# Softmax denominators in a four-batch attention layer: row sums by matmuls with ones, or by 32x32 transposes and row sums on VectorE

## The chip, the cores and the metric

The kernel runs on one core of one Trainium2 chip. The metric is the device time of one execution in microseconds (us). The engines that matter are TensorE (PE in the profile; its weight loads are listed apart as PEld), VectorE (DVE), ScalarE (ACT), GpSimd (POOL), and SyncE (SP), which issues nearly all the DMAs. Each engine executes its own instructions in the order in which the program issued them, so an instruction that has to wait holds up everything behind it on the same engine.

## The reference

The layer is a group norm, a projection to queries, keys and values, attention over 48x48 = 2304 positions with 8 heads of 64 channels, an output projection and a residual sum, for 4 images of 512 channels.

```
hn = _group_norm(x, gn_scale, gn_bias)
qkv = jnp.einsum('oc,bchw->bohw', qkv_w, hn) + qkv_b[None, :, None, None]
qkv = qkv.reshape(b, 3, num_heads, d, t).astype(jnp.float16)
q, k, v = (qkv[:, 0], qkv[:, 1], qkv[:, 2])
scale = jnp.asarray(1.0 / math.sqrt(math.sqrt(d)), dtype=jnp.float16)
w = jnp.einsum('bhct,bhcs->bhts', q * scale, k * scale)
w = jax.nn.softmax(w, axis=-1)
a = jnp.einsum('bhts,bhcs->bhct', w, v).astype(jnp.float32)
a = a.reshape(b, c, hh, ww)
out = jnp.einsum('oc,bchw->bohw', proj_w, a) + proj_b[None, :, None, None]
return x + out
```

The change is about the denominator of the softmax: for each head and query, the sum of the exponentials over all 2304 keys.

## The kernel before

**Tiling.** Heads are worked on in pairs, one head on partitions 0 to 63 and the other on 64 to 127; there are 16 pairs (4 images, 4 pairs each). The queries of a pair are cut into five blocks, four of 512 columns and one of 256. The keys are cut into 18 tiles of 128. A unit is one step of the main loop (L1332): the scores of three 1024-column tiles for a block, their exponentials, and so on. A block of 512 has six units, one of 256 has three, so there are 27 units to a pair and 432 in all, and 80 blocks.

**One iteration n of the main loop**, in order of issue:

- `scores(n)` (L920): matmuls of keys and queries into a PSUM tile `ps` (three buffers), and three exponentials on ScalarE (L939) from it into an fp16 tile `p` with room for three units.
- `add(n-1)` (L968): VectorE adds the unit's `p` to the block's running fp16 sum `acc` (L986, 3072 columns). At the last unit of a block the three thirds are joined into the first one by two further additions (L989). After this, `acc` holds, for each of the 128 partitions (keys modulo 128), 1024 partial sums: two heads by 512 queries.
- `values(n-2)` (L942): matmuls of `p` and the values into the only `av` bank. After a block's last unit VectorE copies the bank out (`avx`, L966).
- `fill(n)` (L1283): a ration of other work that keeps TensorE busy: projections for the queries and keys of later pairs (L709, evacuated at L719), for the values (L760, L768), the output projection (L837, L864). All of these chains use one PSUM bank, `pw` (`ps_w` has one buffer), so the first matmul of a chain waits until VectorE has evacuated the chain before. A chain of 512 columns of a projection is issued in two halves over two iterations, and the evacuation comes at the end of the second. `fill` also releases small VectorE tasks at certain stages: statistics of the next image (L608) and its normalization (L660).

**The sums**, for a block whose last unit is n-2. In iteration n+1, ahead of `scores`, `add_up` (L992) multiplies `acc` by a matrix of ones on TensorE: two matmuls of 512 columns (four of 256 for the narrow block), which put each head's sum on all 64 of its partitions, into the `av` bank. `rows` (L1021) copies that bank to SBUF on VectorE (`slx`, L1025) and sends one row of each head by DMA to a [128, 2, 4] tile `sums`. In iteration n+2, after `values`, GpSimd compares the sums with two limits (`check_sums`, L1040), and VectorE takes the reciprocals (`invert`, L1050), which go by DMA to a row in DRAM. In n+3 `spread` reads that row back, broadcast over partitions (`ib`), and in n+4 `divide` multiplies `avx` by it on GpSimd (L1073). In iteration n+1 `fill` is issued ahead of `values`, since the next block's `values` need the `av` bank that `slx` still has to be copied out of.

The last three of the 80 blocks (`soon` and the very last one, L1326) have a path of their own and keep the matmuls with ones.

Of the kernel before, what the change touches and what calls it, by code (L numbers as in the profile page):

```python
# [12 lines left out]
F32 = mybir.dt.float32  # L13
# [4 lines left out]
ALU = mybir.AluOpType  # L18
AX = mybir.AxisListType
# [7 lines left out]
P = 128  # L27
# [6 lines left out]
BEHIND = 2  # L34
# [8 lines left out]
QB = 512  # L43
QBLOCKS = [(o, min(QB, T - o)) for o in range(0, T, QB)]
# [4 lines left out]
SUM_MIN, SUM_MAX = 256.0, 60000.0  # L49
# [418 lines left out]
def fast_path(  # L468
# [12 lines left out]
    nc = tc.nc  # L481

    RES = NC
    const = ctx.enter_context(tc.tile_pool(name="const", bufs=1))
    xpool = ctx.enter_context(tc.tile_pool(name="xpool", bufs=1))
    qkp = ctx.enter_context(tc.tile_pool(name="qkp", bufs=3))
# [3 lines left out]
    work = ctx.enter_context(tc.tile_pool(name="work", bufs=2))  # L490
    small = ctx.enter_context(tc.tile_pool(name="small", bufs=2))
    dram = ctx.enter_context(tc.tile_pool(name="dram", bufs=4, space=DRAM))
# [7 lines left out]

    SPARE = {(1, 2): lambda c: ("res", RES), (1, 3): lambda c: (f"a32_{c}", 1)}

# [71 lines left out]
    ones16 = const.tile([P, D], F16, name="ones16")  # L574
    nc.gpsimd.memset(ones16, 1.0)

    fine = const.tile([P, 2 * QB // P], F32, name="fine")
    nc.gpsimd.memset(fine, 1.0)

# [14 lines left out]

    SQ = 32
    NGROUP = SQ // GROUP  # L600
    moments = const.tile([P, 3, SQ], F32, name="moments")
    nc.gpsimd.memset(moments, 1.0)
# [303 lines left out]

    open_sums = set()
    av, acc, pts, avx, sums, rowd, ibs = {}, {}, {}, {}, {}, {}, {}  # L910

    stream = []
# [7 lines left out]
    def scores(u):  # L920
        g, j, k, _ = u
        o, n = QBLOCKS[j]
        per = QB // n
        qt, kt = qk[g]
        pt = ppool.tile([P, BURST, 2, QB], F16, tag="p", name=f"p_{g}_{j}_{k}")
        for r in range(BURST):
            ps = ps_s.tile([P, 2, QB], F32, tag="ps", name=f"ps_{g}_{j}_{k}_{r}")
            for a in range(per):
                i = (k * BURST + r) * per + a
                for h in range(2):  # L930
                    rows = slice(h * D, (h + 1) * D)
                    nc.tensor.matmul(  # L932
                        ps[:, h, a * n : (a + 1) * n],
                        kt[rows, bass.ts(i, P)],
                        qt[rows, o : o + n],
                        start=True,
                        stop=True,
                    )
            nc.scalar.activation(pt[:, r], ps, AF.Exp)  # L939
        pts[u] = pt  # L940
# [27 lines left out]
    def add(u):  # L968

        g, j, k, last = u  # L970
        pt = pts[u]
        if k == 0:
            acc[g, j] = [pt]
            return
        if j >= NQ - 2 and g == NG - 1 and (last or j == NQ - 1):
            acc[g, j].append(pt)
            return
        before = acc[g, j][0]
        if k == 1:
            acc[g, j] = [  # L980
                work.tile(
                    [P, BURST, 2, QB], F16, tag="acc", bufs=1, name=f"acc_{g}_{j}"
                )
            ]
        t = acc[g, j][0]
        nc.vector.tensor_tensor(t, before, pt, ALU.add)  # L986
        if last:
            for r in range(1, BURST):
                nc.vector.tensor_tensor(t[:, 0], t[:, 0], t[:, r], ALU.add)  # L989
            acc[g, j] = [t[:, :1]]  # L990

    def add_up(g, j, bank=None, more=False):  # L992


        o, n = QBLOCKS[j]
        per = QB // n
        sl = bank
        if bank is None:
            sl = ps_av.tile([P, QB], F32, tag="av", name=f"sl_{g}_{j}")
        steps = [  # L1000
            (t, r, a)
            for t in acc.pop((g, j))
            for r in range(t.shape[1])
            for a in range(per)
        ]
        for i, (t, r, a) in enumerate(steps):
            for h in range(2):
                lo = h * D
                nc.tensor.matmul(  # L1009
                    sl[lo : lo + D, :n],  # L1010
                    ones16,
                    t[:, r, h, a * n : (a + 1) * n],
                    start=(i == 0 and (g, j) not in open_sums),
                    stop=(i == len(steps) - 1 and not more),
                )
        if more:
            acc[g, j] = []
            open_sums.add((g, j))
        return sl

    def rows(g, j, sl):  # L1021

        o, n = QBLOCKS[j]
        sx = work.tile([P, QB], F32, tag="rows", name=f"slx_{g}_{j}")
        nc.vector.tensor_copy(sx[:, :n], sl[:, :n])  # L1025
        sm = small.tile([P, 2, QB // P], F32, tag="sums", name=f"sums_{g}_{j}")
        for h in range(2):
            nc.sync.dma_start(sm[:, h, : n // P], sx[h * D : h * D + 1, :n])
        sums[g, j] = sm
        return sx  # L1030

    def divide_here(g, j, source, products, engine):
        o, n = QBLOCKS[j]
# [6 lines left out]
    def check_sums(g, j):  # L1040
        n = QBLOCKS[j][1]
        sm = sums[g, j][:, :, : n // P]
        ok = fine.rearrange("p (h i) -> p h i", h=2)[:, :, : n // P]
        for op, limit in ((ALU.is_ge, SUM_MIN), (ALU.is_le, SUM_MAX)):
            t = small.tile([P, 2, QB // P], F32, tag="in", name=f"in_{g}_{j}")
            t = t[:, :, : n // P]
            nc.gpsimd.tensor_scalar(t, sm, limit, None, op)  # L1047
            nc.gpsimd.tensor_tensor(ok, ok, t, ALU.mult)

    def invert(g, j):  # L1050
        n = QBLOCKS[j][1]
        per = n // P
        inv = small.tile([P, 2, QB // P], F32, tag="inv", name=f"inv_{g}_{j}")
        nc.vector.reciprocal(inv[:, :, :per], sums[g, j][:, :, :per])
        row = dram.tile([2, QB], F32, tag="row", name=f"row_{g}_{j}")
        nc.sync.dma_start(
            row[:, :n].rearrange("h (p i) -> p h i", i=per), inv[:, :, :per]
        )
        rowd[g, j] = row
# [103 lines left out]
    for b in range(B):  # L1163
        g = b * NPAIR
# [163 lines left out]
    def block_at(n):  # L1328

        return stream[n][:2] if ended(n) and n not in soon else None  # L1330

    for n in range(end):  # L1332
        now[0] = n
        while loads and loads[0][0] <= n:
            loads.popleft()[1]()
        summed = block_at(n - BEHIND - 1)
        if summed:
            rows(*summed, add_up(*summed))
        wanted(stream[n][0])
        scores(stream[n])  # L1340
        if n > 0:
            add(stream[n - 1])
        if summed:

            fill(n)
        if n >= BEHIND:
            values(stream[n - BEHIND])
        if block_at(n - BEHIND - 2):
            check_sums(*block_at(n - BEHIND - 2))
            invert(*block_at(n - BEHIND - 2))  # L1350
        if block_at(n - BEHIND - 3):
            spread(*block_at(n - BEHIND - 3))
        if block_at(n - BEHIND - 4):

            divide(*block_at(n - BEHIND - 4))
        if not summed:
            fill(n)
        if n - BEHIND in soon:
            g, j = stream[n - BEHIND][:2]
            sx = rows(g, j, add_up(g, j))  # L1360
            if n - BEHIND == soon[1]:
                divide_here(g, j, sx, avx[g, j], nc.gpsimd)
        if n - BEHIND - 1 == soon[0]:
            check_sums(g, j)
            invert(g, j)
        if n - BEHIND - 2 == soon[0]:
            spread(g, j)
            divide(g, j)
    g, b, j = NG - 1, B - 1, NQ - 1
    n = QBLOCKS[j][1]  # L1370
# [5 lines left out]
    sl = ps_s.tile([P, 2, QB], F32, tag="ps", name="sl_last")[:, 0, :]  # L1376
# [2 lines left out]
    values(stream[-1])  # L1379
    add_up(g, j, sl)  # L1380

    every = fine.shape[1] + n
    fines = work.tile([P, QB], F32, tag="rows", name="fines")[:, :every]
    ok = work.tile([P, QB], F32, tag="avx", name="ok")[:, :n]
    nc.scalar.copy(fines[:, :n], sl[:, :n])
    nc.gpsimd.tensor_scalar(ok, fines[:, :n], SUM_MIN, None, ALU.is_ge)
    nc.gpsimd.tensor_scalar(fines[:, :n], fines[:, :n], SUM_MAX, None, ALU.is_le)
    nc.gpsimd.tensor_tensor(fines[:, :n], fines[:, :n], ok, ALU.mult)
    nc.gpsimd.tensor_copy(fines[:, n:], fine)
    divide_here(g, j, sl, av[0], nc.vector)  # L1390
    att32(b, j, LAST)
    while beside or loads:
# [10 lines left out]
    good = small.tile([P, 1], F32, tag="good", bufs=1, name="good")  # L1403
    pf = small_bank("count")[:1, :1]
    for i, (evacuate, store) in enumerate(ends_of):
        if i == NC - 1:
            nc.vector.tensor_reduce(good, fines, AX.X, ALU.add)
            nc.tensor.matmul(pf, good, ones, start=True, stop=True)
        if i == len(rest) - 1:
            nc.vector.tensor_scalar(flag, pf, P * every - 0.5, None, ALU.is_lt)  # L1410
        evacuate()
        store(nc.scalar if i % 2 else nc.sync)
# [57 lines left out]
```

## Time and profile before

| what | value |
|---|---|
| timed runs | median 1619.79 us of 3, 1617.14 to 1620.52 |
| span of the profiled execution, first to last instruction | 1617.1 us |
| the profiled execution's time around its span | none is listed apart; the lowest timed run (1617.14) equals the span |
| chain that ended last, by engine | PE 91%, ACT 4%, issue 2%, DVE 1%, DMA 1% |
| exponentials, L939 | 1296 of 1027 ns |
| additions to `acc`, L986 | 270 of 1798 ns and 79 of 1749 ns |
| joins, L989 | 156 of 695 ns |
| HBM | 49 GB/s over the span |

Busy time of an engine is the union of its instructions' times; the matmuls overlap each other in the pipeline, so the mean of one is longer than its share of the time. The chain of work is followed back from the last instruction: it names the engine that the end waited for. Starts in a timeline are us from the start of the span.

### The profile page before, as it was taken

The page shows a single profiled execution, that of the slowest core. Times are in us where ns is not written, and L with a number is a line of the kernel's source. Part 1 is how long each engine was busy: PE and PEld are TensorE (multiplying, and loading weights), DVE is VectorE, ACT ScalarE, POOL GpSimd, SP SyncE. Part 2 cuts the span into 40 slices and gives each one's busy share as a digit, 9 for nine tenths or more (in the row PEclk, how much of TensorE's full clock was granted, in tenths as well). Part 3 has the DMA queues.
Part 4 walks back from the last instruction along what each step waited for, and adds up shares of the span by engine and source line. Part 5 has one row for each costly group of instructions (what it writes and reads, how often), then busy time and mean ns, then how long its engine had stood idle before and what let it go on. Part 6 is the DMA issues. An engine that isn't in the chain of part 4 may idle for free.

```text
span 1617.1 us, 28315 instructions
## 1 busy us (share of the span) xinstructions
PE 1583.4 (98%) x11500; PEld 695.5 (43%) x11500; DVE 1136.2 (70%) x1302; ACT 1282.8 (79%) x1398; POOL 298.4 (18%) x419
## 2 busy tenths in 40 slices
PE   6999999999999999999999999999999999999996
PEld 2533434443333534555333353455533334434544
DVE  6267668866666678986666666898666666767775
ACT  3077777888888888888887887887888888888894
POOL 1001102211121222212111121111211131111211
PEclk9999999999999999999999999999999999999999
DMA  7002020000000023511000002352100000016424
GB/s 221 1 14 66 11 64 24 18 14 11 14 18 14 12 65 118 154 54 28 14 11 18 14 12 61 100 158 73 31 14 12 14 18 15 15 24 191 121 62 132
DMA packets 94898, 82.11 MB, mean 51 GB/s; under 512 B 50852, under 2 KB 60964, under 8 KB 94756
## 3 DMA queue, kind: packets, MB, share of 16 engines
q1 hardware_dynamic: 92724, 78.35, 17.3%
q8 instruction: 92, 1.51, 0.4%
q10 hardware_dynamic: 1904, 1.84, 0.4%
q14 instruction: 50, 0.41, 0.1%
q0 software_dynamic: 128, 0.01, 0.0%
HBM read 60.70 MB, written 19.17 MB: 49 GB/s over the span
## 4 chain that ended last, share of the span: by engine, by line
PE 91%; ACT 4%; issue 2%; DVE 1%; DMA 1%; POOL 0%; SPq 0%; ACTq 0%; DVEq 0%; POOLq 0%
PE pqk L709 29%; PE ps L932 19%; PE av L957 19%; PE pv L760 16%; PE pr L837 7%; ACT p L939 3%; PE ps L709 1%; PE sl L1009 1%; ACT a L831 1%; DMA x<-x_dram 1%; DVE acc L986 0%; DMA sums<-slx 0%; DVE r L860 0%; DMA row<-inv 0%; DMA ib<-row 0%
## 5 line engine op out<-in xcount | busy, mean ns | idle before, releaser
L939 ACT ACTIVATE p<-ps 128x1024 f16<-128x1024 f32 x1296 | 1231.9, 1027 | 299.9 <-PE ps L932 299.3
L986 DVE TENSOR_TENSOR acc<-acc,p 128x3072 f16<-128x3072 f16 x270 | 485.3, 1798 | 75.5 <-ACT p L939 74.7
L709 PE MATMUL pqk<-x,wqkv 128*64 128x512 f32 (+1 forms) x2464 | 519.3, 551 | 0.0
L932 PE MATMUL ps<-q,k 64*128 64x512 f16 (+1 forms) x2880 | 359.5, 358 | 6.2 <-ACT p L939 5.3
L957 PE MATMUL av<-p,v 128*64 128x512 f16 (+1 forms) x2880 | 361.0, 364 | 0.4 <-DVE slx L1025 0.3
L760 PE MATMUL pv<-wqkv,x 128*64 128x256 f32 x2304 | 268.6, 380 | 0.0
L709 PEld LDWEIGHTS pqk<-x,wqkv 128*64 128x64 f32 x2464 | 168.9, 137 | 224.2 <-issue 166.8
L1047 POOL TENSOR_SCALAR in<-sums 128x8 f32<-128x8 f32 (+1 forms) x158 | 116.6, 738 | 795.0 <-DMA sums<-slx 788.7
L932 PEld LDWEIGHTS <-k 64*128 64x128 f16 x2880 | 107.3, 94 | 286.1 <-issue 238.1
L957 PEld LDWEIGHTS <-v 128*64 128x64 f16 x2880 | 131.9, 109 | 210.8 <-issue 166.6
L1073 POOL TENSOR_TENSOR att<-avx,ib 128x512 f16<-128x512 f32 (+1 forms) x78 | 120.0, 1539 | 450.4 <-DMA ib<-row 406.3
L760 PEld LDWEIGHTS pv<-wqkv,x 128*64 128x64 f32 x2304 | 160.1, 137 | 92.8 <-issue 4.5
L986 DVE TENSOR_TENSOR acc<-p,p 128x3072 f16<-128x3072 f16 x79 | 138.2, 1749 | 0.0
L837 PE MATMUL pr<-a,whi 128*128 128x512 f32 (+1 forms) x312 | 122.2, 399 | 4.6 <-DVE r L860 3.2
L837 PE MATMUL pr<-a,wlo 128*128 128x512 f32 (+1 forms) x312 | 114.4, 373 | 0.0
L989 DVE TENSOR_TENSOR acc<-acc 128x1024 f16<-128x1024 f16 x156 | 108.4, 695 | 5.4
L719 DVE TENSOR_SCALAR q<-pqk,bqkv 128x512 f16<-128x512 f32 (+1 forms) x79 | 55.0, 696 | 80.4 <-PE pqk L709 79.8
L719 DVE TENSOR_SCALAR k<-pqk,bqkv 128x512 f16<-128x512 f32 (+1 forms) x75 | 52.2, 696 | 78.1 <-PE pqk L709 78.0
L768 DVE TENSOR_TENSOR v<-pv,bv 128x512 f16<-128x512 f32 x72 | 49.7, 691 | 81.1 <-PE pv L760 80.9
L966 DVE COPY avx<-av 128x512 f32<-128x512 f32 (+1 forms) x79 | 50.6, 641 | 66.4 <-PE av L957 66.4
L864 DVE SCALAR_TENSOR_TENSOR r<-pr,bproj,r 128x512 f32<-128x512 f32 (+1 forms) x80 | 54.9, 694 | 43.6 <-PE pr L837 43.0
L837 PEld LDWEIGHTS pr<-a,whi 128*128 128x128 f32 x312 | 58.5, 187 | 41.9 <-issue 18.7
(62 smaller groups left out, 448.8 us busy)
## 6 DMA issues: line engine op xcount, KB each, us to landing
r<-x_dram SPq DMA_DIRECT2D x72, 256.0 KB, 3.0
out_dram<-r SPq DMA_DIRECT2D x69, 256.0 KB, 2.1
ib<-row SPq DMA_DIRECT2D x126, 128.0 KB, 3.0
x<-x_dram SPq DMA_DIRECT2D x62, 256.0 KB, 4.3
x<-x_dram SPq DMA_DIRECT2D x16, 128.0 KB, 4.8
sums<-slx SPq DMA_DIRECT2D x128, 2.0 KB, 2.1
ib<-row SPq DMA_DIRECT2D x30, 64.0 KB, 3.0
wqkv<-qkv_wT_dram SPq DMA_DIRECT2D x2, 768.0 KB, 6.9
```

The lines of the kernel that those rows point to most:

```text
L709: nc.tensor.matmul(pw[0][lo : lo + D, :n], wqkv[:, c, w0 + lo : w0 + lo + D], hn[b, c, j], start=(c == 0), stop=(c == NC - 1),)
L719: nc.vector.tensor_scalar(qk[g][part][:, o : o + n], pw[0][:, :n], bqkv[:, col : col + 1], SCALE, ALU.add, ALU.mult,)
L760: nc.tensor.matmul(pw[0][lo : lo + D, a, :], hn[b, c, i * P // QB][:, at + lo : at + lo + D], wqkv[:, c, 2 * C + half * C // 2 :][:, : C / ...
L837: nc.tensor.matmul(ps[:, :n], w[:, c, bass.ts(m, P)], at32[b, j, c], start=(i == 0), stop=(i == len(steps) - 1),)
L864: nc.vector.scalar_tensor_tensor(xt[:, i], places[i], bias, xt[:, i], ALU.add, ALU.add)
L932: nc.tensor.matmul(ps[:, h, a * n : (a + 1) * n], kt[rows, bass.ts(i, P)], qt[rows, o : o + n], start=True, stop=True,)
L939: nc.scalar.activation(pt[:, r], ps, AF.Exp)
L957: nc.tensor.matmul(av[0][lo : lo + D, :n], vv[b, pr // 2][:, i, pr % 2 * P + lo : pr % 2 * P + lo + D], pt[:, r, h, a * n : (a + 1) * n], ...
L986: nc.vector.tensor_tensor(t, before, pt, ALU.add)
L989: nc.vector.tensor_tensor(t[:, 0], t[:, 0], t[:, r], ALU.add)
L1047: nc.gpsimd.tensor_scalar(t, sm, limit, None, op)
L1073: nc.gpsimd.tensor_tensor(atts[g][:, o : o + n], avx.pop((g, j))[:, :n], ibs.pop((g, j))[:, :n], ALU.mult,)
```

## The change

For 77 of the 80 blocks the matmuls with ones, the copy `slx` and the two DMAs of rows go. In their place:

- `turn`, in iteration n, after `scores(n)` and ahead of the copy `avx`: VectorE transposes the 128 x 1024 fp16 sums in 32x32 squares, into the second third of the same `acc` tile (free after the joins).
- `fold`, at the end of iteration n, after `fill`: VectorE sums each run of 32 columns of the transposed tile (128 x 1024 fp16 into 128 x 32 fp32). Four DMAs bring the four groups of 32 partitions of the result side by side on 32 partitions (`quarters`, 32 x 128).
- `invert_turned`, in iteration n+2, where `invert` stood: VectorE sums the four quarters (and, for the narrow block, its two halves), takes 32 reciprocals on 32 partitions, and transposes the 32x32 square; for the narrow block GpSimd first sets the unused columns to one. Two DMAs instead of one write the row to DRAM. The comparisons on GpSimd follow here, on 32 partitions.

`spread` and `divide` stay where they were; so does the order of `fill` and `values` in iteration n+1.

```diff
     for n in range(end):
         now[0] = n
...
         summed = block_at(n - BEHIND - 1)
-        if summed:
-            rows(*summed, add_up(*summed))
         wanted(stream[n][0])
         scores(stream[n])
+        if block_at(n - BEHIND):
+            turn(*block_at(n - BEHIND))
         if n > 0:
             add(stream[n - 1])
         if summed:
...
         if block_at(n - BEHIND - 2):
-            check_sums(*block_at(n - BEHIND - 2))
-            invert(*block_at(n - BEHIND - 2))
+            invert_turned(*block_at(n - BEHIND - 2))
...
         if not summed:
             fill(n)
+        if block_at(n - BEHIND):
+            fold(*block_at(n - BEHIND))
```

The new functions:

```python
    def turn(g, j):

        nc.vector.transpose(
            t_turned(g, j).rearrange("p h n -> p (h n)"),
            acc[g, j][0][:, 0].rearrange("p h n -> p (h n)"),
        )

    def fold(g, j):

        part = small.tile([P, SQ], F32, tag="part", name=f"part_{g}_{j}")
        nc.vector.tensor_reduce(
            part,
            t_turned(g, j).rearrange("p h (c k) -> p (h c) k", k=SQ),
            AX.X,
            ALU.add,
        )
        del acc[g, j]
        quarters = small.tile([SQ, P // SQ, SQ], F32, tag="quarters", name=f"qs_{g}_{j}")
        for p in range(P // SQ):
            nc.sync.dma_start(quarters[:, p, :], part[bass.ts(p, SQ), :])
        sums[g, j] = quarters

    def t_turned(g, j):
        return acc[g, j][0][:, 1]

    def invert_turned(g, j):
        n = QBLOCKS[j][1]
        per, cols = QB // n, n // SQ
        quarters = sums.pop((g, j))
        sm = small.tile([SQ, 2, cols], F32, tag="tsum", name=f"tsum_{g}_{j}")
        nc.vector.tensor_reduce(
            sm,
            quarters.rearrange("i p (h a c) -> i h c p a", h=2, a=per),
            AX.XY,
            ALU.add,
        )
        inv = small.tile([SQ, SQ], F32, tag="tinv", name=f"tinv_{g}_{j}")
        if 2 * cols < SQ:
            nc.gpsimd.memset(inv[:, 2 * cols :], 1.0)
        nc.vector.reciprocal(inv[:, : 2 * cols], sm.rearrange("i h c -> i (h c)"))
        back = small.tile([SQ, SQ], F32, tag="tback", name=f"tback_{g}_{j}")
        nc.vector.transpose(back, inv)
        row = dram.tile([2, QB], F32, tag="row", name=f"row_{g}_{j}")
        for h in range(2):
            nc.sync.dma_start(
                row[h, :n].rearrange("(c i) -> c i", i=SQ),
                back[h * cols : (h + 1) * cols, :],
            )
        rowd[g, j] = row
...
```

The rest of the change keeps books: the joined `acc` tile is kept whole, so that its second third can be written, and the flags of the comparisons get 32 more columns on 32 partitions.

## The prediction, made before the changed kernel was run

> **What bounds the kernel now.** I read the busy shares and slices first, then the groups by shape, then one block's end in the timeline, then the busy time by stage.
>
> ```profile
> PE 1583.4 (98%) x11500; PEld 695.5 (43%) x11500; DVE 1136.2 (70%) x1302; ACT 1282.8 (79%) x1398; POOL 298.4 (18%) x419
> DVE  6267668866666678986666666898666666767775
> ```
>
> TensorE is busy without a gap between the first and the last slice, so each microsecond taken from it can shorten the run. VectorE has 30% to spare on average, but three stretches with an 8 or 9. The groups by shape (busy us, mean ns | idle before) show what goes and the nearest prices:
>
> ```profile
> L1025 DVE COPY slx<-sl 128x512 f32<-128x512 f32 x64 | 43.8, 684 | 19.1 <-PE sl L1009 19.1
> L1009 PE MATMUL sl<-acc,ones 128*64 128x512 f16 x132 | 25.2, 383 | 0.2 <-DVE avx L966 0.2
> L1054 DVE RECIPROCAL inv<-sums 128x8 f32<-128x8 f32 x63 | 12.3, 195 | 0.0
> L622 DVE STREAM_TRANSPOSE turned<-moments 128x96 f32<-128x96 f32 x7 | 2.2, 307 | 0.2
> L645 DVE STREAM_TRANSPOSE cols<-both 128x64 f32<-128x64 f32 x7 | 1.7, 245 | 0.2
> L1407 DVE TENSOR_REDUCE good<-fines 128x1 f32<-128x264 f32 x1 | 0.4, 418 | 0.0
> ```
>
> The timeline (start, length) of a block's end near 1180 us:
>
> ```profile
> 1176.08 0.82 PE L932 MATMUL ps<-q,k 64*128 64x512 f16 x6
> ...
> 1177.78 0.69 DVE L966 COPY avx<-av 128x512 f32<-128x512 f32 x1 [0.95 <-PE av L957]
> ...
> 1179.22 0.38 PE L1009 MATMUL sl<-acc,ones 128*64 128x512 f16 x2
> 1179.44 0.75 DVE L719 TENSOR_SCALAR k<-pqk,bqkv 128x512 f16<-128x512 f32 x1 [0.97 <-PE pqk L709]
> 1179.54 0.82 PE L932 MATMUL ps<-q,k 64*128 64x512 f16 x6
> 1180.11 0.68 DVE L1025 COPY slx<-sl 128x512 f32<-128x512 f32 x1
> 1180.29 0.20 PEld L709 LDWEIGHTS pqk<-x,wqkv 128*64 128x64 f32 x4 [0.42 <-DVE k L719]
> 1180.29 1.94 PE L709 MATMUL pqk<-x,wqkv 128*64 128x512 f32 x8
> ```
>
> The point is the `k` evacuation: it ends at 1180.19, and the next chain, which needs the same bank, starts at 1180.29. The sums' matmuls and the scores are what TensorE does meanwhile; the cover is nearly used up. Last, busy time by stage:
>
> ```profile
> 600.00:720.00 120.00, 118.94 (x812) 57.68 (x810) 105.02 (x139) 102.99 (x120) 25.14 (x31) 1.00 0.39 116
> 720.00:1020.00 300.00, 300.00 (x2240) 123.46 (x2236) 204.32 (x209) 247.56 (x261) 59.87 (x80) 1.00 0.10 23
> 1020.00:1120.00 100.00, 97.27 (x650) 49.17 (x648) 86.35 (x117) 85.06 (x101) 19.09 (x26) 1.00 0.42 128
> ```
>
> (length; busy PE, PEld, DVE, ACT, POOL; clock; DMA share; GB/s). VectorE is 68% busy in a plain stage, but 86 to 88% where the next image's statistics and normalization run; 240 to 340 us is like that too, at 84%.
>
> [...] The trace has fp32 transposes alone, 245 ns for 64 columns and 307 for 96. [...]
>
> **Part by part.** *Matmuls removed.* In the timeline above the scores start at 1176.08, 1179.54 and, in the next iteration, 1182.81; an iteration with the same fill and no block end takes 3.24 us (scores at 714.97 and 718.21), this one 3.46. So a block's sums cost TensorE 0.215 us (narrow blocks the same: four matmuls of half length). Beside output projections the step is larger (3.93 against 3.59 at 1055 us): 0.34 at 12 blocks. 65 x 0.215 + 12 x 0.34 = 18.1 us. That is the whole gain; the weights of ones loaded under cover.
>
> *VectorE per block.* Removed: `slx` 0.68 and the reciprocal 0.20. [...]
>
> *First fill of iteration n+1.* Without the sums the scores start 0.215 earlier, so the fill at 1180.29 would start at 1180.07; its bank is free at 1180.19, plus 0.06 for the signal: 1180.25. So 0.18 of 0.215 is lost to a wait that the removed matmuls had covered. For a `v` evacuation (0.69) 0.12 is lost, after an output projection 0.16, and nothing where no chain ends there (26 blocks) or it is narrow. Outside the crowded stages: 30 blocks, 5.0 us. `turn` delays nothing here, since VectorE stands idle 0.95 before `avx`, which then ends at 1178.83, before 1179.44.
>
> *`fold`.* It runs behind the evacuation: 1180.22 to 1181.43, where `slx` ended at 1180.79. The first `add` of the next block so ends at 1183.10, not 1182.46; the exponentials that reuse its `p` buffer start at 1183.24. A margin of 0.14 remains, so ScalarE isn't held.
>
> *Quarters and `invert_turned`.* The DMAs of sums take 0.54 us each to issue and land 2.1 after issue; four take 3 x 0.55 + 2.1 = 3.75, landing at 1185.2. VectorE comes there at 1184.9, waits 0.3, and is through at 1186.05; the next evacuation, at 1186.16, is not late. But ahead of each narrow block's end the same 0.8 us stands between the joins and an evacuation with 0.5 to spare: seven such places at 0.5, 3.5 us outside the crowded stages. On GpSimd the narrow block's fill with ones stands behind the previous block's division, which now ends 1.6 us before that reciprocal and will be some 1.5 later: nothing, up to 0.5 us at 15 blocks. SP issues three more DMAs a block, 1.5 us of a 20 us block; its own loads come iterations ahead.
>
> *Crowded stages.* There the tasks follow `avx` and precede the evacuation, so `turn` pushes it. Near 648 us: the joins end at 644.99, an evacuation and `turn` reach 647.6, `avx` 648.3 (was 647.26), two statistics 649.7, and the evacuation, formerly 648.57 to 649.32, ends at 650.41. The projection at 649.55 waits till 650.47 instead of coming at 649.21: 1.2 us lost for 0.34 won. I walked through these stages in that manner, each VectorE instruction no earlier than its input and the one ahead of it: 2.4 us at 100 to 160, 5.0 at 240 to 335, 7.3 at 600 to 720, 7.5 at 1020 to 1140, 22 in all. [...] TensorE has 1.1 and 2.7 us of idle time there that can absorb some; I take 20.
>
> Sum: -18.1 + 5.0 + 3.5 + 20 = +10.4 us on the profiled 1617.1, so 1627.5. The median is 2.7 above that execution: **1630 us**.
>
> **Unknown costs, both ends.** [...] Landing of the quarters 0.75 later, as in stages full of loads: +5. GpSimd's wait: +1. Neither DMA can go below nothing, since no one waits for sums on TensorE now.
>
> **Rivals.**
> - *The matmuls' time is simply won.* For it: TensorE bounds the whole middle, VectorE has 480 us free. Against: the evacuation at 1180.19. If tasks absorb the crowding and it costs 3 instead of 20, 1619.8 - 18.1 + 5 + 3.5 + 3 = 1613. This ends on the other side; it decides if VectorE's added time in the crowded stages is below about 1 us a block beyond what is free. Chance 0.2.
> - [...] Chance 0.1.
> - [...] Chance 0.12.
> - *VectorE held by late quarters or by GpSimd*, everything behind it late: +17 to +22, 1640. For it loads at 128 GB/s in the crowded stages. Chance 0.13.
> - *Forecast*, own range 1624 to 1637: 0.45.
>
> The change does do what it says for 77 blocks; nothing in the order leaves matmuls with ones behind. Faster or slower means beyond 0.2%, 3.2 us, about what a measurement can tell here: faster 0.2, same 0.1, slower 0.7. The range 1609 to 1650 takes in all but most of the two-cycle case and the pure gain of 1602.
>
> **What would show it.** The matmuls with ones (L1009) fall from 234 to 50; `turn` near 1.25 us, `fold` near 1.2; VectorE near 1325 us; TensorE idle before L709, L760 and L837 with an evacuation (L719, L768, L864) as releaser, in short waits at plain blocks and waits near 1 us at 280, 650 to 700 and 1030 to 1110. Wrong if the crowded stages are no longer than before, or if `turn` is far from 1.25.

## The result, and the profile after

The changed kernel takes 1627.0 us (median of 4, 1624.67 to 1627.33) where the kernel before takes 1619.22 on the same chip (4 runs): a ratio of 1.0046, with a 95% interval of 1.0032 to 1.0060. It is slower by about 7.8 us. The profiled execution has a span of 1625.6 us against 1617.1, so +8.5; its own time is 1627.3, so 1.7 us lie around a span. (It is 1.7 to 1.9 in all runs here; that the lowest time of the kernel before equals its span is chance.)

The busy shares and VectorE's slices of the profile after:

```profile
PE 1574.3 (97%) x11316; PEld 685.0 (42%) x11316; DVE 1319.5 (81%) x1533; ACT 1283.2 (79%) x1398; POOL 236.2 (15%) x434
DVE  6278789978788889998778787999878887888885
```

TensorE has 9.1 us less to do and still ends later: it now waits. The new groups, by shape (busy us, mean ns | idle before, and what ended it):

```profile
L1036 DVE STREAM_TRANSPOSE acc<-acc 128x1024 f16<-128x1024 f16 x77 | 94.9, 1232 | 0.6
L1044 DVE TENSOR_REDUCE part<-acc 128x32 f32<-128x1024 f16 x77 | 92.8, 1205 | 0.0
L1064 DVE TENSOR_REDUCE tsum<-qs 32x32 f32<-32x128 f32 x62 | 22.4, 361 | 4.8 <-DMA qs<-part 4.6
```

`turn` (L1036) and `fold` (L1044) cost what was forecast, 1.25 and 1.21. The waits of TensorE's weight loads on the evacuations of the one `pw` bank, before and after (us in total, times, longest):

```profile
PEld pqk L709 <- DVE k L719: 5.5, 14, 0.4
PEld pqk L709 <- DVE q L719: 4.2, 11, 0.4
PEld pr L837 <- DVE r L864: 4.2, 10, 0.7
```

```profile
PEld pqk L711 <- DVE k L721: 16.6, 27, 1.6
PEld pqk L711 <- DVE q L721: 9.9, 18, 1.8
PEld pr L839 <- DVE r L866: 14.6, 25, 1.8
DVE tsum L1064 <- DMA qs<-part: 5.3, 8, 1.6
```

These are the three waits with the evacuations of `k`, `q` and the residual sums: 13.9 us before, 41.1 after (for `v` it is 2.8 and 8.5). They are idle times of the weight loads; the matmuls lose a part of each. The last line is new: VectorE itself waits for the quarters, eight times.

One block's end in a plain stage shows both kinds of loss. Timeline of the kernel after (start, length, the idle time ahead of it and what ended that):

```profile
827.89 0.75 DVE L721 TENSOR_SCALAR k<-pqk,bqkv 128x512 f16<-128x512 f32 x1 [2.08 <-PE pqk L711]
...
828.70 0.20 PEld L711 LDWEIGHTS pqk<-x,wqkv 128*64 128x64 f32 x4 [0.60 <-DVE k L721]
...
829.79 2.44 SPq L1053 DMA_DIRECT2D qs<-part  x4
...
835.07 0.36 DVE L1064 TENSOR_REDUCE tsum<-qs 32x32 f32<-32x128 f32 x1 [1.57 <-DMA qs<-part]
...
835.97 0.70 DVE L721 TENSOR_SCALAR k<-pqk,bqkv 128x512 f16<-128x512 f32 x1
...
836.72 1.94 PE L711 MATMUL pqk<-x,wqkv 128*64 128x512 f32 x8 [0.68 <-DVE k L721]
```

At 828.70 the chain waits for the evacuation that the matmuls with ones had covered: the first-fill wait of the prediction. The weight load stands idle for 0.60 us; of TensorE's time some 0.2 go, since the scores are 3.45 us apart there (827.77 and 831.22) and 3.23 in the next iteration. At 836.72 TensorE loses 0.68 us more, two iterations later: the quarters, issued from 829.79 on, let the small sum start at 835.07, 5.3 us after `fold` ended; the sum, the reciprocals and the small transpose then stand ahead of the `k` evacuation. Its matmuls had ended at 834.52, while VectorE stood idle for the quarters: VectorE kept to the order of issue.

In a crowded stage the second kind is there although the quarters come in time:

```profile
669.91 0.43 SPq L812 DMA_DIRECT2D r<-x_dram  x1
...
671.31 0.38 DVE L1064 TENSOR_REDUCE tsum<-qs 32x16 f32<-32x128 f32 x1
...
672.20 0.69 DVE L614 BATCH_NORM_AGGREGATE moments<-st 128x2 f32<-128x30 f32 x4
...
674.50 0.75 DVE L866 SCALAR_TENSOR_TENSOR r<-pr,bproj,r 128x512 f32<-128x512 f32 x1 [0.34 <-DMA r<-x_dram]
...
675.30 0.50 PE L839 MATMUL pr<-a,whi 128*128 128x512 f32 x1 [1.20 <-DVE r L866]
```

The three small instructions push the statistics, and these push the residual sum `r`. VectorE is through with them at 674.15 and then waits 0.34 us more for a load of the residual, which SP had issued at 669.91, behind the four issues of the quarters (666.80 to 669.24). The output projection stands still for 1.20 us, and the scores are 5.25 us apart where they were 4.15. The busy time by stage (length; busy PE, PEld, DVE, ACT, POOL; clock; DMA share; GB/s):

```profile
600.00:720.00 120.00, 114.65 (x756) 54.25 (x754) 113.47 (x149) 99.95 (x117) 17.60 (x30) 1.00 0.38 119
720.00:1020.00 300.00, 297.19 (x2208) 122.44 (x2208) 241.40 (x257) 247.13 (x260) 42.82 (x82) 1.00 0.08 22
1020.00:1120.00 100.00, 95.61 (x617) 46.32 (x614) 96.58 (x129) 85.06 (x102) 12.73 (x27) 1.00 0.43 133
```

VectorE is at 95 and 97% in the crowded windows, and TensorE, which had 118.94 and 97.27 there, has 114.65 and 95.61.

To place the difference I added up, from the traces, the times from one unit's scores to the next one's, against the same units of the kernel before. "Crowded" are the units that start there at 100 to 165, 240 to 345, 600 to 725 and 1020 to 1145 us. The kernel after has +9.1 us in these (0.9, 3.0, 4.3, 0.9) and -1.1 in all the rest. So what the removed matmuls gave is used up outside, and the crowded stages add the loss. Each such figure is from one execution of each kernel, so it is good to a microsecond or two. What lies ahead of the first scores and behind the last ones is not in these sums. It is +0.5 us here, but +2.7 in e1 and +2.0 in e2 below; why it is more there stays open.

### The profile page after: what moved, and what is told of

Its sections match the earlier page's. It is cut to its first block, busy times and chain, and to the rows that moved or that the text cites. A ratio compares the mean times of both kernels' runs of the same rounds, so it can differ in the third digit from the quotient of the medians.

```text
span 1625.6 us, 28473 instructions
## 1 busy us (share of the span) xinstructions
PE 1574.3 (97%) x11316; PEld 685.0 (42%) x11316; DVE 1319.5 (81%) x1533; ACT 1283.2 (79%) x1398; POOL 236.2 (15%) x434
## 4 chain that ended last, share of the span: by engine, by line
PE 72%; DVE 15%; ACT 4%; DMA 4%; issue 3%; SPq 2%; POOL 0%; DVEq 0%; ACTq 0%; POOLq 0%
PE pqk L711 26%; PE av L959 14%; PE pv L762 14%; PE ps L934 14%; DVE acc L988 4%; PE pr L839 3%; ACT p L941 3%; DVE part L1044 2%; PE ps L711 1%; SPq L1053 1%; DMA qs<-part 1%; DVE r L866 1%; DVE acc L991 1%; DMA r<-x_dram 1%; DVE k L721 1%
## 5 line engine op out<-in xcount | busy, mean ns | idle before, releaser
L1086 POOL TENSOR_SCALAR tin<-tsum 32x32 f32<-32x32 f32 (+1 forms) x154 | 45.0, 292 | 953.1 <-DVE tsum L1064 947.9
L1036 DVE STREAM_TRANSPOSE acc<-acc 128x1024 f16<-128x1024 f16 x77 | 94.9, 1232 | 0.6
L1044 DVE TENSOR_REDUCE part<-acc 128x32 f32<-128x1024 f16 x77 | 92.8, 1205 | 0.0
```

The lines of the kernel that those rows point to most:

```text
L1036: nc.vector.transpose(t_turned(g, j).rearrange("p h n -> p (h n)"), acc[g, j][0][:, 0].rearrange("p h n -> p (h n)"),)
L1044: nc.vector.tensor_reduce(part, t_turned(g, j).rearrange("p h (c k) -> p (h c) k", k=SQ), AX.X, ALU.add,)
```

## The experiments

All are edits of the kernel after; the numbers of units' times given below are against the kernel before, as above. The kernel before took 1618.2 to 1618.9 us beside them.

### What the removed matmuls are worth: e1 and e2

```diff
-        if block_at(n - BEHIND):
-            turn(*block_at(n - BEHIND))
...
-            invert_turned(*block_at(n - BEHIND - 2))
+            del acc[block_at(n - BEHIND - 2)]
+            sums[block_at(n - BEHIND - 2)] = fixed
+            check_sums(*block_at(n - BEHIND - 2))
+            invert(*block_at(n - BEHIND - 2))
...
-        if block_at(n - BEHIND):
-            fold(*block_at(n - BEHIND))
```

e2 issues `values` ahead of `fill` in every iteration besides:

```diff
-        if summed:
-            fill(n)
         if n >= BEHIND:
             values(stream[n - BEHIND])
...
-        if not summed:
-            fill(n)
+        fill(n)
```

> Leaves out the sums of the 77 blocks: a constant tile is inverted in their place, as before; no matmuls with ones, no copy out of PSUM, and no transposes or row sums on VectorE. Theory (VectorE's added work and its place cost the time, and the bank's evacuation loses its cover): the full gain of 18.1 us less the waits of the first fill at plain blocks (5 to 8 us, no added work in the crowded stages): 1606 to 1609. Rival (the matmuls' time is simply won once VectorE's work is away): 1601. Rival (the matmuls with ones were never on the path): 1617 to 1620.

> As the run before, sums of 77 blocks left out, and in the iteration after a block's end the values' matmuls are issued ahead of the fill, as in all other iterations. Theory: the values' matmuls (0.67 us) cover the evacuation of the bank, so the whole gain comes: 1600 to 1602, 5 to 7 us below the run before. Rival (no wait for the bank in the first fill): the same time as the run before.

e1: 1608.53 us, ratio 0.9938 (0.9923 to 0.9953). e2: 1600.65, 0.9889 (0.9874 to 0.9904). Both are in the range expected; the step between them, 7.9, is a little over the 5 to 7. The matmuls' time, together with that of the copies `slx`, which go too, is 17.6 us where nothing replaces them and the order covers the bank's evacuation; the forecast had 18.1. Leaving `fill` first costs 7.9 of it. By stages that is 5.6 us outside the crowded ones (-13.0 against -7.4; forecast 5.0) and 1.5 within (-6.4 against -4.9).

### The complete computation with that wait taken away: e3

The edit is the second diff above, alone.

> The changed kernel with values ahead of fill in the iteration after a block's end, nothing left out. Theory: the waits of the first fill (some 10 us in the trace, at the unit with k=2 of each block) go, those two iterations later (some 8 us, k=4) and ahead of the narrow block's end (4 us) stay: 1616 to 1619. Rival (VectorE's total or late quarters hold everything, so a wait removed in one place comes back in the next): 1624 to 1627.

1622.28 us, 1.0026 (1.0017 to 1.0035), between the two ranges: only 4.7 of the 7.9 us came back. The trace says why. Sorted by their place in a block, the intervals in which the first fill's wait fell are back to -0.1 us over the 64 wide blocks (the kernel after had +9.2), but the intervals in which `invert_turned` is issued rose from +8.0 to +11.7. Something that hangs on the invert step takes back what is won ahead of it.

### The invert step one iteration later: e4

```diff
-        if block_at(n - BEHIND - 2):
-            invert_turned(*block_at(n - BEHIND - 2))
         if block_at(n - BEHIND - 3):
-            spread(*block_at(n - BEHIND - 3))
+            invert_turned(*block_at(n - BEHIND - 3))
         if block_at(n - BEHIND - 4):
-            divide(*block_at(n - BEHIND - 4))
+            spread(*block_at(n - BEHIND - 4))
+        if block_at(n - BEHIND - 5):
+            divide(*block_at(n - BEHIND - 5))
```

> The changed kernel with invert_turned, spread and divide one iteration later each, nothing left out. Theory that VectorE stands waiting for late quarters, with an evacuation behind it: the waits at k=4 fall from 8 us to 2 or less and some of those ahead of the narrow block's end move: 1619 to 1622. Rival (only the length of the three small instructions counts, wherever they stand): 1625 to 1628. Rival (only the first fill's wait counts): 1627.

1637.08 us, 1.0116 (1.0101 to 1.0132), a clear miss. The intervals of the old place fell from +8.0 to +2.1, but two others rose, from +9.2 to +12.9 and from +0.9 to +8.4. There is a new wait, of VectorE on GpSimd's filling of the unused columns with ones, which now stands behind a division:

```profile
DVE tback L1075 <- POOL tinv L1072: 12.3, 13, 3.4
```

And the edit moved more than the small step: the division on GpSimd, one iteration later too, now falls beside VectorE's joins of the next block.

```profile
1210.23 1.51 POOL L1130 TENSOR_TENSOR att<-avx,ib 128x512 f16<-128x512 f32 x1 [3.03 <-DMA ib<-row]
1210.64 2.37 DVE L991 TENSOR_TENSOR acc<-acc 128x1024 f16<-128x1024 f16 x2
```

The two joins take 2.37 us here, 1.42 at the same place in the kernel after. Over the whole trace of e4, 57 of the 156 joins overlap a division by more than 0.1 us and take 1418 ns in the mean; the other 99 take 692, none over 694. In the kernel after 3 overlap. That is 41 us of VectorE's time, just ahead of the evacuations at a block's end: the intervals behind the ends of the wide blocks lose 8.6 us against the kernel after, of 10.1 in all. A version that moves the small step and leaves the division where it was wasn't tried.

### The transpose and the row sum alone: e10 and e6

The prediction made `turn` the cause of its largest term. e10 is e1 with `turn` and `fold` put back where the kernel after has them; the four DMAs and the three small instructions are left out, and the values are divided by the inverse of a constant. e6 is the same with e3's order. Against e1 the main loop of e10 has:

```diff
+        if block_at(n - BEHIND):
+            turn(*block_at(n - BEHIND))
...
+        if block_at(n - BEHIND):
+            fold(*block_at(n - BEHIND))
```

> The changed kernel's own order (fill ahead of values), with the large transposes and row sums, but a constant inverted as before, no gathering DMAs and no small instructions (denominators of 77 blocks left out). If, as the prediction has it, the large transposes push the evacuations of the crowded stages: 1618 or more. If they cost as little as with values ahead of fill (2.9 us) or twice that: 1610 to 1615.

> The version with values ahead of fill, with the large transposes and row sums kept, but without the four DMAs and the three small instructions; a constant is inverted as in the kernel before, so the denominators of 77 blocks are left out. Theory: what the invert step and its wait cost (k=4 and ahead of narrow blocks' ends) goes, and the 2.45 us of large instructions cost only what they push in the crowded stages: 1603 to 1608. Rival (the large instructions are the cost, in crowded stages): 1612 or more.

e10: 1610.76 us, 0.9950 (0.9935 to 0.9965), far below the 1618 of the prediction's view. e6: 1603.51, 0.9905 (0.9890 to 0.9920). So 77 transposes and 77 sums of 1.2 us each, 174.6 us of VectorE's time by e6's and e2's totals (1268.4 against 1093.8), cost 2.2 and 2.9 us of the kernel's. By stages e10 loses 3.4 us against e1 in the crowded ones and 0.6 elsewhere (e1 lost 3 us more than e10 outside the units, so the spans differ by 0.9 only).

### The three small instructions alone, and both: e12 and e8

e8 is e3 whose small sum reads a constant, without the four DMAs; e12 is e8 without `turn` and `fold`.

```diff
-        quarters = small.tile([SQ, P // SQ, SQ], F32, tag="quarters", name=f"qs_{g}_{j}")
-        for p in range(P // SQ):
-            nc.sync.dma_start(quarters[:, p, :], part[bass.ts(p, SQ), :])
-        sums[g, j] = quarters
+        sums[g, j] = part
...
-        quarters = sums.pop((g, j))
+        del sums[g, j]
+        quarters = fixed.unsqueeze(1).to_broadcast((SQ, P // SQ, SQ))
```

> Values ahead of fill; the three small VectorE instructions read a constant, and the four gathering DMAs are left out too (the denominators of 77 blocks are left out). Theory that the three instructions' 0.9 us, in the queue ahead of an evacuation, cost what is left (1619.7 us with the DMAs against 1603.5 without either): 1616 to 1620. Rival (the four DMAs a block on SP's queue, which delay the loads behind them): 1604 to 1608.

> e8 without the transpose and the fold: the three small instructions read a constant, no gather DMAs, values ahead of the fill. The sums of the 77 blocks are left out, the sums of exponentials that divide their values are a constant. With e2 (1600.7, neither), e6 (1603.5, transpose and fold) and e8 (1616.1, both) this closes a square. If the small instructions cost by themselves, by their place ahead of an evacuation, this gives 1612 to 1614. Rival: the cost comes from both together, VectorE's time per block being too much for the crowded stages; then the small instructions alone cost little, 1602 to 1605.

e8: 1616.06 us, 0.9986 (0.9978 to 0.9993). e12: 1603.56, 0.9908 (0.9893 to 0.9923). e8 came out where its theory had it, and yet e12 has the rival's value: the small instructions' place alone is not the cost. The four runs close a square in one order:

| | no small instructions | small instructions |
|---|---|---|
| no `turn`, `fold` | e2 1600.65 | e12 1603.56 (+2.9) |
| `turn` and `fold` | e6 1603.51 (+2.9) | e8 1616.06 (+15.4) |

Each part by itself costs 2.9 us, both together 15.4: 9.6 us belong to neither, but to their meeting. (The runs were made on three chips; by the ratios to the kernel before beside each they are 3.1, 2.6 and 15.7.) With the small instructions come a second DMA of the row and GpSimd's comparisons in their new form, and the sum of a constant takes 267 ns where that of the quarters takes 361. By stages, the excess over the sum of the two is 5.5 us in the crowded ones (e2 -6.4, e6 -3.4, e12 -4.5, e8 +4.0) and 3.2 elsewhere (-13.0, -11.9, -11.2, -6.9).

Elsewhere there is a place in each pair where two blocks' work falls together, the end of the narrow block. Timeline of e8, VectorE and TensorE's fill:

```profile
375.32 1.42 DVE L993 TENSOR_TENSOR acc<-acc 128x1024 f16<-128x1024 f16 x2
376.66 0.27 DVE L1064 TENSOR_REDUCE tsum<-fixed 32x32 f32<-32x128 f32 x1
...
377.47 0.70 DVE L723 TENSOR_SCALAR k<-pqk,bqkv 128x512 f16<-128x512 f32 x1
378.10 1.22 DVE L1038 STREAM_TRANSPOSE acc<-acc 128x1024 f16<-128x1024 f16 x1
```

```profile
378.22 1.95 PE L713 MATMUL pqk<-x,wqkv 128*64 128x256 f32 x16 [0.55 <-DVE k L723]
```

The wide block's small instructions follow the narrow block's joins; the evacuation that TensorE wants comes 0.8 us later for them, and `turn` is queued behind. From 370.36, where the wide block's `fold` starts, to 379.63 VectorE has no gap above 0.1 us. The scores stand 3.25 us apart here in e2, 3.58 in e6, 3.39 in e12 and 4.03 in e8: once more than the sum of the two.

### The DMAs of the quarters, and the wait for them: e5

e5 is e3 whose small sum reads a constant (the second half of the diff above), while the four DMAs are still issued.

> The version with values ahead of fill (1622.3 us), but the first of the three small VectorE instructions reads a constant instead of the gathered quarters, so the denominators of 77 blocks are left out; the four DMAs are still issued. Theory that VectorE waits for late quarters: the waits at k=4 (11.7 us there) fall to about 5: 1614 to 1617. Rival (only the 0.9 us that the three instructions take ahead of an evacuation count): 1620 to 1623.

1619.65 us, 1.0006 (0.9998 to 1.0015), just below the rival's 1620 to 1623 and far from the theory's 1614 to 1617. Waiting for the landing is worth at most 2.6 us (e3 less e5; the sum of the constant is also 0.09 us shorter in each block), having the four DMAs in SP's queue 3.6 (e5 less e8). By the ratios both are 3.2, and e5's twelve runs lie between 1616 and 1623, so the two can't be told apart in size. In the crowded stages the units lose +9.1, +6.5 and +4.0 us in e3, e5 and e8; 1.6 of e3's can be TensorE's clock, which was 0.60 in the mean of 697 to 701 us there.

### Other places for the small step: e11, e9, e7

e11 keeps the complete computation in e3's order and puts `invert_turned` behind `fill`:

```diff
-        if block_at(n - BEHIND - 2):
-            invert_turned(*block_at(n - BEHIND - 2))
...
         fill(n)
+        if block_at(n - BEHIND - 2):
+            invert_turned(*block_at(n - BEHIND - 2))
```

> The complete computation of the changed kernel, with the values ahead of the fill as in e3 and `invert_turned` issued behind `fill`, next to the fold, so that it stands behind an iteration's evacuation instead of ahead of it. If the place of the three small instructions ahead of an evacuation is what the invert step costs, most of the 16 us of the step goes: 1604 to 1612, faster than both kernels, and VectorE's waits by position show no loss two iterations after a block's end. Rival: VectorE's total and the DMAs hold it, and the wait only moves one instruction on (the joins, the scale or the next evacuation come late): 1618 to 1622.

1620.89 us, 1.0016 (1.0007 to 1.0024), in the rival's range. It is the fastest complete version tried, 6 us ahead of the kernel after, and still not ahead of the kernel before. Outside the crowded stages the move does what was hoped (-8.4 us where e3 has -3.6), within them it loses 2 more (+11.1 against +9.1; the profiled execution is 2.1 us slower than the median). At one place there two things come together; timeline of e11, then its window of the 4 us that follow:

```profile
694.95 0.75 DVE L866 SCALAR_TENSOR_TENSOR r<-pr,bproj,r 128x512 f32<-128x512 f32 x1 [2.82 <-DMA r<-x_dram]
...
695.75 0.50 PE L839 MATMUL pr<-a,whi 128*128 128x512 f32 x1 [2.45 <-DVE r L866]
```

```profile
697.00:701.00 4.00, 4.00 (x20) 1.50 (x20) 4.00 (x5) 3.29 (x6) 2.36 (x3) 0.57 0.55 172
```

VectorE waits 2.82 us for a load of the residual that SP had issued at 689.71, behind the quarters, and that landed at 694.82. TensorE stands 2.45 us, and then its clock is 0.57 in the mean of 4 us. In the whole trace 17 joins lie beside a division, which makes them 14 us longer in all.

e9 transposes `part` right behind `fold`, lets GpSimd add the quarters, has VectorE take the reciprocals one iteration later, and `spread` and `divide` one later too; e7 has GpSimd also invert, by raising to the power -1, so that nothing small is left on VectorE but the transpose. Of e7's edit:

```diff
+        flat = small.tile([P, SQ], F32, tag="flat", name=f"flat_{g}_{j}")
+        nc.vector.transpose(flat, part)
...
+        nc.gpsimd.tensor_tensor(quarters[:, :2], quarters[:, :2], quarters[:, 2:], ALU.add)
...
+        nc.gpsimd.tensor_tensor(sm, quarters[:, 0], quarters[:, 1], ALU.add)
+        nc.gpsimd.tensor_tensor(inv, sm, minus, ALU.pow)
```

> Computes everything: values ahead of fill; row sums transposed on VectorE right after they are made; GpSimd adds the gathered quarters; VectorE takes the 32 reciprocals one iteration later (0.35 us, nothing to wait for), spread and divide one later each. If the small instructions' time on VectorE is the cost: 1605 to 1612, faster than both kernels. If the four DMAs are: 1616 to 1620.

> A version that computes everything: values ahead of fill; the 128x32 row sums are transposed once on VectorE right after they are made (0.2 us), the four DMAs gather them with the queries along the row, and GpSimd adds the quarters and takes the inverses, so that VectorE neither waits for a DMA nor does anything two iterations later. If the invert step on VectorE is what is left: 1605 to 1610, faster than both kernels. Rival (VectorE's total in the crowded stages, or GpSimd slowing VectorE): 1616 or more.

e9: 1624.54 us, 1.0035 (1.0023 to 1.0047). e7: 1650.42, 1.0203 (1.0189 to 1.0217). e9 is above both of its ranges; e7 is far from the gain hoped for, and its rival had only said 1616 or more. e9 has only -4.8 us outside the crowded stages and +11.3 within, 9.4 of them at 600 to 725, where two intervals near 666 and 693 us lose more than 3 each behind late residual sums; behind these stalls TensorE's clock was 0.57 in the mean of 670 to 674 us and again of 697 to 701, which can account for up to 1.7 us of each loss (0.43 of 4 us). And e9 has e4's trouble: 60 of its joins lie beside a division and take 1449 ns, 45 us more in all, and the intervals behind the wide blocks' ends lose 8.7 us against e3. So e9 doesn't show that GpSimd's help is worth nothing. Of e7, a group and a wait:

```profile
L1083 POOL TENSOR_TENSOR qs<-qs,minus 32x32 f32<-32x32 f32 x77 | 425.8, 5530 | 6.0
```

```profile
DVE r L870 <- DMA r<-x_dram: 30.2, 10, 7.9
```

The power takes GpSimd 5.5 us for a 32x32 tile. The DMAs of the row wait for it at the head of SP's queue, the loads of the residual stand behind them, and the `r` evacuations behind those: TensorE waits 41.0 us for `r` in all. (This is e7's fastest execution, at a mean clock of 0.994; the four others had 0.987 to 0.989 and took 3 to 7 us longer.) I had taken GpSimd's time as free because no one reads its results soon; it was SP's queue that made others wait for it.

## Why the prediction came out right, and which of its steps did not

The forecast, 1630 with its own range of 1624 to 1637, holds the 1627.0, and the forecast's side was right. On the span it said +10.4, and +8.5 came; between the profiled span and the median it had put 2.7 us, and 1.4 was measured. That the sum came so near is in part luck: the matmuls were worth a little more, the invert step cost more outside the crowded stages, and the largest term was too high and put down to `turn` first of all. Its terms, with what the runs showed; the measured losses are by stages, each step taken from the one ahead of it (e2, e1, e10, after). They add up to +8.0:

| term | forecast | measured |
|---|---|---|
| matmuls gone | -18.1 | -19.4 (e2; by the medians -17.6) |
| first fill waits, outside the crowded stages | +5.0 | +5.6 (e1 less e2) |
| `invert_turned` ahead of evacuations, outside | +3.5 | +5.7 (after less e10) |
| `turn` and `fold`, outside | 0 | +0.6 (e10 less e1) |
| crowded stages, all causes | +20 | +15.5 (after less e2) |

- *Durations.* `turn` 1.25 against 1.232, `fold` 1.21 against 1.205, VectorE 1325 against 1319.5 us in all, in the mean 2.38 more for each of the 77 blocks (1319.5 less 1136.2). The terms +3.5 and +20 were worked out with lengths of the new instructions that nothing in the profile of before shows; they were the author's estimates, and what the runs showed in their place is 1232 and 1205 ns for the two large instructions and 0.90 us for the three small ones (361, 341 and 199 ns, wide blocks), where the prediction had 0.8. The two fp32 transposes of the kernel before (245 ns for 64 columns, 307 for 96) are 1.94 ns a column apart, by which 1024 columns would have taken 2.1 us; the fp16 transpose took 1.232, so this slow case did not come.
- *First fill.* Right in mechanism and size; the wait at 828.70 is it, and e2 against e1 shows that the order makes it.
- *Crowded stages: the step that failed.* The prediction said "There the tasks follow `avx` and precede the evacuation, so `turn` pushes it", and priced that at 20 by walking through. `turn` and `fold` alone cost 3.4 us there (e10), and 1.5 more are the lost cover of the bank; the other 10.6 come only with the invert step and its DMAs. (Counted in the other order, with values first, the small instructions cost about 2 and `turn` and `fold` on top of them about 8.5, by e12 and e8: the meeting can't be booked to one of them.) By stages the walk-through had 2.4, 5.0, 7.3 and 7.5, and 1.6, 4.4, 5.6 and 3.9 were lost. Its own example, the projection near 649 us, was to come 1.2 us late; in the kernel after TensorE waits 0.32 us there:

```profile
654.19 0.48 PE L839 MATMUL pr<-a,whi 128*128 128x512 f32 x1 [0.32 <-DVE r L866]
```

The walk-through had taken over an addition that lasted 2.18 us in that one trace, with a division beside it; it takes 1.75 now. It also reads the joins there as ending at 644.99, where the second one starts, without harm to its result. What does hold there is VectorE's capacity: 600 to 720 us has six blocks, and with the mean of 2.38 us a block its 105.0 us become 105.0 + 6 x 2.38 = 119.3 of the 120. The square shows that neither part is dear, but the two together.
- *Quarters and `invert_turned`: one place right, one missed.* The narrow blocks' ends cost what was said: of the 16 pairs, six outside the crowded stages lose 0.5 to 0.7 us each, 3.6 in all (after less e10), where seven places and 3.5 us were forecast. What was missing is the interval two iterations behind the first fill, where 2.4 us go outside the crowded stages: the four issues took 2.44 us and the sum could start 5.3 us after `fold` in the block shown, not 3.75; VectorE waited up to 1.6 us, not 0.3. (The 0.54 us an issue was low already for the kernel before, whose median is 0.59.) In the values-first order the landing costs up to 2.6 and the DMAs' place in SP's queue 3.6, where the prediction had nothing for either.
- *Margins.* ScalarE was held after all: 26 waits for `add`, 18.7 us. It passed nothing on, since the scores waited 5.1 us for exponentials where they had 5.3. GpSimd's fill with ones was free, as said, and became a cost in e4.
- *The rival that the matmuls' time is simply won* (1613) named its own condition, less than about 1 us a block beyond what is free in the crowded stages. e6 and e10 show it nearly met by the two large instructions, 1603.5 and 1610.8; with the gather and the inversion besides it isn't met.

What remains open: why two small parts that cost 2.9 us each cost 15.4 together is shown as a fact of place and stage; that it is the missing gaps, and not one particular instruction, is argued from the timelines. e8 with shorter transposes would test it and wasn't tried. Nor was a version like e9 that keeps the divisions away from the joins. No complete version that keeps the sums on VectorE beat the kernel before.

## What to carry to other kernels

A matmul that is taken off the bounding engine may have been the cover of somebody's evacuation: price the removal by what TensorE would wait for next, and look first whether another order of issue gives the cover back (7.9 us here for two lines). When work moves to an engine with idle time on average, add up all of it in the stage where that engine is fullest, the small dependent instructions and their DMAs included, since parts that fit one by one need not fit together. And before handing a slow step to an idle engine, ask which queue will stand still until it is done, and when moving a step in the order, look at what it then runs beside: VectorE's joins that had a division on GpSimd beside them took 1418 ns in e4 and 1449 in e9, where the others of e4 took 692.

## What the runs showed of the hardware that was not expected

- VectorE's additions of two fp16 tiles of 128x1024 took 692 ns, and 1418 in the mean while GpSimd multiplied fp32 tiles of up to 128x512 beside them (e4, 99 and 57 of them). In the fourteen traces 173 of these additions took over 0.9 us, and all had such a multiplication beside them.
- Raising a 32x32 fp32 tile to a power took 5530 ns on GpSimd (e7), where VectorE's reciprocals of the same tile take 341 ns.
- Behind some stalls of TensorE its clock was lower: in e11, behind a stall of 2.45 us, it was 0.57 in the mean of 697 to 701 us, and the matmuls there came every 0.43 us instead of 0.23; in e9, behind one of 1.53 us, it was 0.57 in the mean of 670 to 674, and they came every 0.43 too. A stall alone does not decide: near the end, behind the same wait of 3.2 us for `r`, the matmuls came every 0.23 us in the kernel before and every 0.43 in e2.
- Four DMAs of 4 KB from SBUF to SBUF took 0.61 us each to issue in the block shown (0.58 in the median of all), and what stood in SP's queue behind them cost no less (3.6 us) than the wait for their data (2.6 at most).
